# A scan stage on VectorE: partial sums taken up one step later, a sixth buffer for them, and source tiles placed at other points of TensorE's queue

## The chip, the cores and the metric

The kernel runs on one core of a Trainium2 chip. A core has a matrix engine (PE; its weight loads are shown as PEld), a vector engine (DVE), a scalar engine for activations and copies (ACT), a general engine (POOL) and a queue engine that issues transfers (SP). Each works through its own queue in order, and they wait for one another by semaphores. The metric is device time in microseconds (us) of one execution: the median of several runs. A profile is one further execution, recorded instruction by instruction.

## The reference

Two layers work on 4096 tokens of 256 numbers. Layer 0 is a graph convolution with a selective scan (Mamba), followed by a mixture of experts; layer 1 has another graph convolution and another mixture. All is float32. The change lies in the first part of layer 0:

```
h = relu(adj @ layernorm(x) @ gcn_w + gcn_b)
h = layernorm(h) * ln_g + ln_b
xz = h @ w_in;  xc, z = xz[:, :512], xz[:, 512:]
u = silu(causal_conv4(xc) + conv_b)
dbc = u @ w_xp;  dt = softplus(dbc[:, :16] @ w_dt + b_dt)
B, C = dbc[:, 16:32], dbc[:, 32:]
state = exp(dt * A) * state + dt * u * B      # per token; 512 channels x 16 states
y = sum over states of (state * C) + u * D_skip
x = x + (y * silu(z)) @ w_out
```

## The kernel before

**Tiles and steps.** The 4096 tokens are cut into 8 chunks of 512. The 512 channels are 4 blocks (`m`) of 128, one channel to a partition, and the 16 states are taken in pairs (`g`). One step is one block with one pair of states, so a chunk has 32 steps: steps 0 to 15 take blocks 0 and 1 in turn over the 8 pairs, steps 16 to 31 blocks 2 and 3. All 256 steps run in one Python loop (L1195), whose order is written out by hand for PE, DVE, ACT and POOL; SP's order is left to the scheduler.

**One step (class `Step`).** For step n, POOL multiplies dt*u by the broadcast row B into `db` (L1105, 128x1024, both states at once). ACT computes the decay exp(dt*A) for each state into a PSUM tile `da` (L1113, two buffers). DVE scans along the 512 tokens, once for each state (L1120), and multiplies by the row C into `hc` (L1130, 128x1024, five buffers). ACT keeps the last column as the state (L1126). In the next step a transfer on POOL's queue adds the second half of `hc` to the first (`pair`, L1134). Later PE multiplies the sum by the identity and adds it up over the 8 pairs in a PSUM bank `psy` (`total`, L1147; two banks, ps_y). The first sum of a block (g = 0: steps 0, 1, 16 and 17) is preceded by the skip product u*D (L1142, weights `dD`). After the eighth (steps 14, 15, 30 and 31), and in the step after its sum, DVE multiplies `psy` by silu(z) in place of u (`gate`, L1156), which frees the bank. A float32 matmul shows as two instructions in the profile.

**Which sum is taken up when.** The loop at L1234 takes up, in step n, the sum of step n-3, so that the transfer of `hc` has about two steps to land. In the last chunk `hc` is not paired (`paired` is false), PE adds both halves, and the sum of step n-2 is taken up at once.

**What runs beside the scan.** While chunk c is scanned, three things are prepared on PE and ACT.

- `propagation(c+2)` multiplies the adjacency by the normalised x. It is a generator of 66 pieces: for each half of the chunk, 32 pieces (one 128-row tile of x; four matmul instructions of 128x256, L644) into the one PSUM bank `pt`, and a 33rd, in which ACT copies the bank into `pts` (L650) and the next half's first matmul must wait for it. The source tiles `at` come by SP in transfers of four pieces each, with three buffers.
- `Front(c+1)` makes the inputs of the next chunk's scan by a plan of steps (`PLAN`, L660): the GCN product in step 8, the transposes `turn` in 12 (PE, L737), `turned` in 13 (ACT, L744, into `hT`), the in-projection `xz` from 13 on (PE, L756), the causal convolution `conv` as products with diagonal matrices (PE, L773), silu into `us` in 17 and 21 (ACT, L783), the projections, dt and softplus. Entries from 32 on are steps 0 to 7 of the next chunk: the gate half of `xz`, its copy into `zs` (L769) and its silu (L780).
- From step 8 of chunk 6 on there is no propagation left. `Tail` does the out-projection of finished chunks there, with the residual x loaded into `xr` (L883), and `Last` that of chunk 7.

**The planner.** The loop at L1164 to L1174 spreads the 66 pieces over the 32 steps. Each step has an estimated cost on PE and on DVE, and each piece goes to the step where PE's cost less DVE's is smallest. `pieces[i]` is the result; steps 3, 8, 13, 15 to 17, 20 and 23 get none, steps 27 and 29 to 31 five each. The call `advance(pieces[i])` comes at a step's end (L1255). The prologue does chunk 0's propagation and `Front(0)`, with pieces of chunk 1 filled in by the table `FILL`.

In step n the loop issues, in this order: inputs of step n+1 (POOL), the pair transfer of n-1 (POOL), the two scans (DVE) and decays of n+1 (ACT), the product (DVE), the gates of sums taken up in step n-1 (DVE), the sums (PE), the plan's entries, `Tail`, and the pieces. The lines in question:

```
while summed < n - 1 and (summed < n - 2 or not steps[summed].paired):
    steps[summed].total()
    gated.append(summed)
    summed += 1
```

Of the kernel before, what the change touches and what calls it, by code (L numbers as in the profile page):

```python
# [9 lines left out]
F32 = mybir.dt.float32  # L10
# [8 lines left out]
P = 128  # L19
CW = 512  # L20
# [8 lines left out]
def kernel(ctx: ExitStack, tc: tile.TileContext, out: bass.AP, **a):  # L29
    nc = tc.nc  # L30
    x, adj, adjT = a["x"], a["adj"], a["adjT"]
    N, D = x.shape
# [508 lines left out]
    with ExitStack() as s1:  # L541
# [76 lines left out]

        PE_RATIO = 1.0
        FILL = {11: 8, 12: 2, 16: 1, 18: 2, 20: 2, 21: 6, 22: 1, 24: 40}  # L620
        PIECE, PE_STEP, DVE_STEP = 1.0, 1.1, 4.3
        PE_COST = {"gcn": 2, "turn": 0.8, "xz": 2, "conv": 4, "project": 2, "dt": 1}
        DVE_COST = {"biased": 0.8, "stats": 1.4, "soft": 2.7}
# [2 lines left out]
        def propagation(c):  # L626


            halves = psts[c] = []
            for r0 in range(c * CW, c * CW + CW, HW):  # L630
                pt = ps_pt.tile([P, DB, HW], F32, name="pt", tag="pt")
                for j4 in range(NT // 4):
                    at = adp.tile([P, 4, HW], F32, name="at")
                    nc.sync.dma_start(
                        at,
                        adjT[j4 * 4 * P:(j4 + 1) * 4 * P, r0:r0 + HW].rearrange(
                            "(j p) i -> p j i", p=P
                        ),
                    )
                    for jj in range(4):  # L640
                        j = 4 * j4 + jj
                        for k in range(DB):

                            nc.tensor.matmul(  # L644
                                pt[:, k, :], xl[:, j, k * P:(k + 1) * P], at[:, jj, :],
                                start=(j == 0 and k == 0), stop=(j == NT - 1 and k == DB - 1),
                            )
                        yield
                pts = w1p.tile([P, DB, HW], F32, name="pts", bufs=2)
                nc.scalar.copy(pts, pt)  # L650
                halves.append(pts)
                yield

        class Front:

# [3 lines left out]

            PLAN = {  # L660
                8: ["gcn 0", "gcn 1"], 9: ["biased 0", "biased 1"], 11: ["normal"],
                12: ["turn 0", "turn 1"], 13: ["turned 0", "turned 1", "xz 0", "xz 1"],
                14: ["in 0", "in 1", "xz 2"], 15: ["conv 0", "in 2"], 16: ["conv 1"],
                17: ["silu 0", "conv 2"], 18: ["xz 3"], 19: ["in 3", "project 0"],
                20: ["conv 3"], 21: ["silu 1"], 22: ["project 1"],
# [75 lines left out]
            def do_turned(self, k):  # L741
                if k == 0:
                    self.hT = w1p.tile([P, DB, CW], F32, name="hT", tag="hT")
                nc.scalar.activation(  # L744
                    self.hT[:, k, :], self.ps.pop(("turn", k)), AF.Identity,
                    bias=ln_b[:, k:k + 1], scale=ln_g[:, k:k + 1],
                )

            def do_xz(self, m):
                if m == 0:  # L750
# [107 lines left out]
        class Tail:  # L858
# [21 lines left out]
                        tails.pop(0)  # L880

            def fetch(self):
                self.xr = w2p.tile([P, 2, D], F32, name="xr")  # L883
                rows = tokens(x, self.c)[:, 2 * self.hh:2 * self.hh + 2, :]
                nc.sync.dma_start(self.xr, rows)
                if self.kept is None:
                    self.y = fronts[self.c].us[:, :, self.hh * HW:(self.hh + 1) * HW]
                else:
                    self.y = adp.tile([P, 4, HW], F32, name="at")
                    nc.sync.dma_start(self.y, self.kept[:, :, self.hh * HW:(self.hh + 1) * HW])  # L890
# [108 lines left out]
        class Last:  # L999
# [6 lines left out]

            def fetch(self):
                for hh in range(2):
                    t = w2p.tile([P, 2, D], F32, name="xr")
                    nc.sync.dma_start(t, tokens(x, NC - 1)[:, 2 * hh:2 * hh + 2, :])  # L1010
                    self.xr.append(t)

# [22 lines left out]
            def norm(self):  # L1035
# [5 lines left out]
                for hh in range(2):  # L1041
# [20 lines left out]
                    for k in range(DB):  # L1062
                        for j in range(2):
                            nc.tensor.transpose(
                                ps_t[:, k, j * P:(j + 1) * P], xn[:, j, k * P:(k + 1) * P], ident
                            )
                    xT = w1p.tile([P, DB, HW], F32, name="pts", bufs=2)
                    nc.scalar.copy(xT, ps_t)
                    for j in range(2):
                        for k in range(DB):  # L1070
# [10 lines left out]
        class Step:  # L1081
# [43 lines left out]
            def product(self):  # L1125
                nc.scalar.copy(  # L1126
                    state[:, self.m, 2 * self.g:2 * self.g + 2], self.db[:, :, CW - 1]
                )
                self.hc = w2p.tile([P, 2, CW], F32, name="hc", bufs=5)
                nc.vector.tensor_tensor(self.hc, self.db, self.cb, ALU.mult)  # L1130

            def pair(self):
# [25 lines left out]
        with tc.manual_schedule(engines={  # L1158
# [8 lines left out]
                    pe[i % STEPS] += PE_COST.get(name.split()[0], 0.0)  # L1167
                    dve[i % STEPS] += DVE_COST.get(name.split()[0], 0.0)
            pieces = [0] * STEPS
            for _ in range(2 * NT + 2):  # L1170
                i = min(range(STEPS), key=lambda i: pe[i] - PE_RATIO * dve[i])
                pieces[i] += 1
                pe[i] += PIECE
            late = sum(pieces[:8])  # L1174

            def advance(k=1):
                for _ in range(k):
                    next(prop, None)

            prop = propagation(0)  # L1180
            advance(NT + 1)
# [9 lines left out]
                advance(k)  # L1191
                left -= k
            advance(left)
            steps, tails, kept, gated, summed = [], [], {}, [], 0
            for n in range(NC * STEPS):  # L1195
                c, i = divmod(n, STEPS)
                if n == 0:
# [33 lines left out]
                for k in gated:  # L1231
                    steps[k].gate()
                gated = []
                while summed < n - 1 and (summed < n - 2 or not steps[summed].paired):  # L1234
                    steps[summed].total()
                    gated.append(summed)
                    summed += 1
# [5 lines left out]
                if c == NC - 1:  # L1243
# [8 lines left out]
                        last.first(0)  # L1252
                    elif i in (27, 28):
                        last.residual(i - 27)
                advance(pieces[i])  # L1255
                cur = nxt
            n = NC * STEPS
            while summed < n:
# [422 lines left out]
```

## Time and profile before

| What | us |
| --- | --- |
| median of three runs (lowest, highest) | 2462.78 (2461.95, 2464.04) |
| the profiled execution, its own time | 2457.31 |
| its span, first to last instruction | 2455.4 |
| prologue, until the first scan | 168.6 |
| scan stage, chunks 0 to 7 | 137.4, 140.4, 140.2, 139.4, 140.4, 140.2, 145.4, 137.9 |
| after the scan (experts, layer 1) | 1158 |
| granted TensorE clock, mean share | 0.957 |

The lengths of chunks and steps are read from the timeline, from the start of one step's first scan on DVE to that of the next. These are the steps of chunks 0 to 6 that matter, in us:

| Step | chunk 0 | 1 | 2 | 3 | 4 | 5 | 6 |
| --- | --- | --- | --- | --- | --- | --- | --- |
| 1 | 3.63 | 3.68 | 3.68 | 3.68 | 3.68 | 3.68 | 3.68 |
| 2 | 3.63 | 4.29 | 4.28 | 4.28 | 4.28 | 4.29 | 4.29 |
| 8 | 5.41 | 5.41 | 5.76 | 6.04 | 5.41 | 5.41 | 5.86 |
| 18 | 4.29 | 5.80 | 5.62 | 4.29 | 5.79 | 5.59 | 6.12 |
| 19 | 4.66 | 4.66 | 4.67 | 4.66 | 4.66 | 4.66 | 6.45 |
| 20 | 3.62 | 3.62 | 3.62 | 3.62 | 3.62 | 3.62 | 3.63 |
| 22 | 5.41 | 5.54 | 5.54 | 5.40 | 5.54 | 5.54 | 5.40 |

Steps 9 to 11, 26, 27, 29 and 30 are longer than 3.7 us because DVE has work of `Front` in them.

How to read the rows: a row of a timeline gives the start in us, the duration, the engine, the line of the kernel, the operation, what it writes and reads, how many instructions are merged, and in brackets the idle time of that engine before it with what ended it. A row of the waits gives who waited for whom, the total in us, how often, and the longest. Matmuls overlap: the time from one start to the next, not the duration, is what one costs PE. At full rate that is 0.215 us for 256 columns and 0.43 us for 512.

### The profile page before, as it was taken

Reading aid. Unit: us, or ns where it says so; the run is one execution under the profiler, and the core shown is the slowest. Engines: PE = TensorE matmul, PEld = TensorE weight load, DVE = VectorE, ACT = ScalarE, POOL = GpSimd, SP = SyncE. Lnnn points to the kernel's source line nnn. Section 1 sums busy time; section 2 is a strip of 40 time slices with the busy share of each in tenths; the row PEclk is TensorE's granted clock in tenths of the full one; section 3 lists DMA queues with packets and bytes.
Section 4 is the critical chain, followed back from the end, with each engine's and each line's share of the span. In section 5 each row is a group of like instructions: output and inputs, shape, how many; then the busy total and the mean of one; then the engine's idle time right before and its main releaser. Section 6 shows DMA issues by size and latency. Waiting matters only on the chain. (4 is left out here: it accounts for less than half of the span.)

```text
span 2455.4 us, 27712 instructions
## 1 busy us (share of the span) xinstructions
PE 2254.5 (92%) x8984; PEld 1635.0 (67%) x8984; DVE 1656.8 (67%) x2377; ACT 1180.5 (48%) x2013; POOL 1142.7 (47%) x831
## 2 busy tenths in 40 slices
PE   5989989999999999997994999979999999999995
PEld 4765655646565564653563888857788888888874
DVE  4049999999999999999898311155366666754233
ACT  1136657465665646566662322224455555633321
POOL 1027677777777677676560555420000000036652
PEclk9989999999999999997995999989999999999998
DMA  6359998989999998998665777743244444457886
GB/s 206 94 158 247 233 272 224 272 219 266 243 241 273 226 271 221 272 241 214 211 211 159 265 227 234 228 143 112 90 147 148 147 146 146 141 158 230 243 284 238
DMA packets 290956, 509.46 MB, mean 207 GB/s; under 512 B 25312, under 2 KB 157536, under 8 KB 289904
## 3 DMA queue, kind: packets, MB, share of 16 engines
q1 hardware_dynamic: 244528, 410.54, 53.9%
q0 software_dynamic: 46272, 97.03, 18.2%
q8 instruction: 75, 1.23, 0.2%
q14 instruction: 81, 0.66, 0.1%
HBM read 406.03 MB, written 42.73 MB: 183 GB/s over the span
## 5 line engine op out<-in xcount | busy, mean ns | idle before, releaser
L1105 POOL TENSOR_TENSOR db<-du,bb 128x1024 f32<-128x1024 f32 x256 | 606.9, 2371 | 357.9 <-ACT state L1126 129.6
L1120 DVE TENSOR_TENSOR_SCAN db<-da,state,db 128x512 f32<-128x512 f32 x512 | 627.4, 1266 | 44.8 <-ACT da L1113 42.6
L1113 ACT ACTIVATE da<-dt,negA 128x512 f32<-128x512 f32 x512 | 347.7, 691 | 358.6 <-DVE db L1120 356.8
L644 PE MATMUL pt<-at,gn 128*128 128x256 f32 x2048 | 488.1, 391 | 34.0 <-DMA at<-in_adjT_dram 27.1
L644 PEld LDWEIGHTS pt<-at,gn 128*128 128x128 f32 x2048 | 398.7, 196 | 164.0 <-issue 74.2
L1405 PE MATMUL pf<-gn,f 128*128 128x256 f32 x2048 | 452.0, 380 | 0.0
L1405 PEld LDWEIGHTS pf<-gn,f 128*128 128x128 f32 x2048 | 387.1, 190 | 56.7 <-issue 6.4
L1130 DVE TENSOR_TENSOR hc<-db,cb 128x1024 f32<-128x1024 f32 x256 | 331.2, 1294 | 17.9
L1147 PE MATMUL psy<-hc,ident 128*128 128x512 f32 x576 | 303.7, 621 | 42.7 <-DMA hc<-hc 38.9
L79 POOL TENSOR_TENSOR ln_rs<-ln_rs,mhalf 128x4 f32<-128x4 f32 (+1 forms) x25 | 33.3, 1331 | 510.6 <-DVE ln_rs L78 450.7
L460 DVE TENSOR_TENSOR yk<-ps_y,bk 128x512 f32<-128x512 f32 x73 | 50.4, 691 | 316.4 <-PE ps_y L455 293.7
L1394 ACT ACTIVATE f<-f 128x1024 f32<-128x1024 f32 x128 | 134.6, 1057 | 194.0 <-DVE f L1393 129.6
L470 PE MATMUL ps_h<-xkT,wk 128*128 128x256 f32 x864 | 212.9, 388 | 10.8 <-DVE xkT L495 7.6
L455 PE MATMUL ps_y<-wk,hk 128*128 128x256 f32 x864 | 211.1, 381 | 0.1
L1134 POOL DMA_DIRECT2D hc<-hc x224 | 195.0, 871 | 0.2
L1147 PEld LDWEIGHTS psy<-hc,ident 128*128 128x128 f32 x576 | 110.0, 197 | 119.9 <-issue 53.2
L470 PEld LDWEIGHTS ps_h<-xkT,wk 128*128 128x128 f32 x864 | 159.5, 193 | 45.4 <-ACT hk L474 11.6
L1393 DVE TENSOR_SCALAR f<-at 128x1024 f32<-128x1024 f32 x128 | 88.0, 688 | 148.3 <-PE pf L1405 134.9
L455 PEld LDWEIGHTS ps_y<-wk,hk 128*128 128x128 f32 x864 | 161.9, 191 | 21.5 <-ACT hk L474 0.9
L1400 DVE SCALAR_TENSOR_TENSOR cnt<-at,cnt 128x1024 bf16<-128x1024 f32 x120 | 145.9, 1216 | 16.4 <-DMA at<-in_adjT_dram 16.1
L474 ACT ACTIVATE hk<-ps_h,d_b 128x256 f32<-128x256 f32 x140 | 66.0, 473 | 184.2 <-PE ps_h L470 184.2
L756 PE MATMUL ps_xz<-hT,w_in 128*128 128x512 f32 x256 | 126.1, 628 | 14.3 <-ACT hT L744 14.3
(305 smaller groups left out, 2569.6 us busy)
## 6 DMA issues: line engine op xcount, KB each, us to landing
at<-in_adjT_dram SPq DMA_DIRECT2D x256, 512.0 KB, 4.4
bb<-bcd SPq DMA_DIRECT2D x128, 512.0 KB, 5.2
cb<-bcd SPq DMA_DIRECT2D x128, 512.0 KB, 4.9
hc<-hc POOLq DMA_DIRECT2D x224, 256.0 KB, 5.3
wk<-in_L_ffn_W_dram SPq DMA_DIRECT2D x70, 512.0 KB, 5.5
wk<-in_L_ffn_expert_w_dram SPq DMA_DIRECT2D x114, 256.0 KB, 4.3
yg<-d_ys SPq DMA_DIRECT2D x14, 512.0 KB, 4.7
yd<-us SPq DMA_DIRECT2D x6, 1024.0 KB, 7.8
```

What stands on the lines that cost most here:

```text
L455: nc.tensor.matmul(ps[:, j, :], hT[:, m, j * P:(j + 1) * P], w[:, m, :], start=(m == 0), stop=(m == kb_out - 1),)
L470: nc.tensor.matmul(ps[:, j, :], w[:, d, m * P:(m + 1) * P], xT[:, d, :], start=(d == 0), stop=(d == DB - 1),)
L644: nc.tensor.matmul(pt[:, k, :], xl[:, j, k * P:(k + 1) * P], at[:, jj, :], start=(j == 0 and k == 0), stop=(j == NT - 1 and k == DB - 1),)
L1105: nc.gpsimd.tensor_tensor(self.db, self.f.du[self.half][:, self.mi:self.mi + 1, :].to_broadcast([P, 2, CW]), self.bb, ALU.mult,)
L1113: nc.scalar.activation(da, self.f.dt[self.half][:, self.mi, :], AF.Exp, scale=negA[:, self.m, n:n + 1])
L1120: nc.vector.tensor_tensor_scan(self.db[:, j, :], da, self.db[:, j, :], state[:, self.m, n:n + 1], ALU.mult, ALU.add,)
L1130: nc.vector.tensor_tensor(self.hc, self.db, self.cb, ALU.mult)
L1134: nc.gpsimd.dma_start(self.hc[:, 0, :], self.hc[:, 1, :], accum_op=ALU.add)
L1147: nc.tensor.matmul(f.psy[m], ident, self.hc[:, j, :], start=False, stop=(self.g == GS - 1 and j == last),)
L1394: nc.scalar.activation(f, f, AF.Square)
L1400: nc.vector.scalar_tensor_tensor(cnt, at, 0.0, cnt, ALU.is_gt, ALU.add)
L1405: nc.tensor.matmul(pf[:, t, :], f[:, jj, t * P:(t + 1) * P], gn[:, j, :], start=(j == 0 and t % 2 == 0), stop=(j == NT - 1 and t % 2 == 1),)
```

## The change

1. The sum of a paired step is taken up in step n+4 instead of n+3, and `hc` has six buffers.
2. A plan entry `fill` in step 13, between `turned` and `xz`, issues two pieces of the propagation (the table `FILLED`). The planner counts them, so 64 pieces are left to spread. Steps 24 and 25 have one piece fewer each (1 and 2 for 2 and 3); all other steps keep theirs. The entry is also met in the prologue.
3. The 33rd piece, the bank copy, ends a step's pieces: what is left over (`owed`) goes to the next step. The first copy falls in step 28 and one piece moves to step 29; the second is the last piece of step 7.
4. To make room, the residual `xr` of `Tail` and `Last` shares the two buffers of `pts`, and the last chunk's transposed tile uses the buffers of `h` and `hT`.

```
+        FILLED = {13: 2}
...
                 nc.scalar.copy(pts, pt)
                 halves.append(pts)
-                yield
+                yield True
...
-                12: ["turn 0", "turn 1"], 13: ["turned 0", "turned 1", "xz 0", "xz 1"],
+                12: ["turn 0", "turn 1"], 13: ["turned 0", "turned 1", "fill", "xz 0", "xz 1"],
...
+            def do_fill(self):
+
+                advance(FILLED[13])
...
-                self.xr = w2p.tile([P, 2, D], F32, name="xr")
+                self.xr = w1p.tile([P, 2, D], F32, name="xr", tag="pts", bufs=2)
...
-                    t = w2p.tile([P, 2, D], F32, name="xr")
+                    t = w1p.tile([P, 2, D], F32, name="xr", tag="pts", bufs=2)
...
-                    xT = w1p.tile([P, DB, HW], F32, name="pts", bufs=2)
+                    xT = w1p.tile([P, DB, HW], F32, name="xnT7", tag=("h", "hT")[hh])
...
-                self.hc = w2p.tile([P, 2, CW], F32, name="hc", bufs=5)
+                self.hc = w2p.tile([P, 2, CW], F32, name="hc", bufs=6)
...
-            for _ in range(2 * NT + 2):
+            for i, k in FILLED.items():
+                pe[i] += k * PIECE
+            for _ in range(2 * NT + 2 - sum(FILLED.values())):
...
-            def advance(k=1):
-                for _ in range(k):
-                    next(prop, None)
+            def advance(k=1, wait=False):
+
+
+                while k > 0:
+                    k -= 1
+                    if next(prop, None) and wait:
+                        break
+                return k
...
-                while summed < n - 1 and (summed < n - 2 or not steps[summed].paired):
+                while summed < n - 1 and (summed < n - 3 or not steps[summed].paired):
...
-                advance(pieces[i])
+                owed = advance(pieces[i] + owed, True)
+                if i == 7:
+                    while owed:
+                        owed = advance(owed, True)
```

## The prediction, made before the result

> **What bounds the kernel now.** I read the page first, then the busy times of windows cut at the chunks of the scan stage, then the waits of each engine inside 165:1297 us, then the timelines of single steps. The scan stage runs from 165 to 1297 us, 256 steps in 8 chunks of 32, and nothing outside it but the prologue is touched. Two rows of the page (instructions and busy time, mean ns, idle before and its releaser) and two chunks as windows (length, busy time of PE, PEld, DVE, ACT, POOL, granted clock, DMA):
>
> ```profile
> L1120 DVE TENSOR_TENSOR_SCAN db<-da,state,db 128x512 f32<-128x512 f32 x512 | 627.4, 1266 | 44.8 <-ACT da L1113 42.6
> L1147 PE MATMUL psy<-hc,ident 128*128 128x512 f32 x576 | 303.7, 621 | 42.7 <-DMA hc<-hc 38.9
> ```
> ```profile
> 446.40:586.60 140.20, 131.47 (x433) 81.56 (x432) 132.49 (x122) 82.70 (x144) 104.06 (x65) 0.98 0.95 248
> 586.60:726.00 139.40, 131.28 (x428) 81.58 (x427) 133.01 (x122) 83.02 (x144) 104.15 (x65) 0.96 0.95 248
> ```
>
> Of a chunk's 140 us DVE works 132.5 and PE 131.5. A step is two scans and one product on DVE, 3.68 us, of which 0.09 is issue; so the stage is DVE's, and PE's idle time, the 38.9 us for the hc transfers among it, costs only what reaches DVE. The waits inside the stage show the way by which it does:
>
> ```profile
> DVE db L1120 <- ACT da L1113: 42.6, 34, 3.9
> ACT xc L763 <- PE ps_xz L756: 20.7, 22, 4.3
> ACT us L783 <- PE ps_xz L773: 13.8, 12, 1.4
> PE psy L1147 <- DMA hc<-hc: 38.9, 17, 5.8
> PE ps_xz L756 <- ACT hT L744: 14.3, 6, 2.9
> ```
>
> DVE waits for almost nothing but the decays da, and ACT is late with those behind its two table loads for a silu, and behind PE. The timeline gives the places: in chunks 1 to 5 DVE stands still in step 8 (1.7 to 2.2 us), step 18 (1.3 to 1.4; 0.09 in chunks 0 and 3) and step 22 (1.7 to 1.9), and next to nowhere else. PE has no idle time from step 15 to step 27: there it works off a backlog that starts with the in-projection xz. PE at that start in chunk 2, then in chunk 3:
>
> ```profile
> 501.61 1.02 PE L1147 MATMUL psy<-hc,ident 128*128 128x512 f32 x2
> 505.54 4.75 PE L756 MATMUL ps_xz<-hT,w_in 128*128 128x512 f32 x7 [2.91 <-ACT hT L744]
> ```
> ```profile
> 641.56 1.80 PE L644 MATMUL pt<-at,gn 128*128 128x256 f32 x4
> 643.16 1.92 PE L1147 MATMUL psy<-hc,ident 128*128 128x512 f32 x2
> 646.36 3.70 PE L756 MATMUL ps_xz<-hT,w_in 128*128 128x512 f32 x8 [1.29 <-ACT hT L744]
> ```
>
> Both start 4.02 us into step 13. After 2.91 us of idling, chunk 2's first matmuls start 1.01, 0.85 and 0.85 us apart; chunk 3's, after 1.29 us, 0.53 and then 0.43. (Chunk 3 had its half rate earlier: the four matmuls at 641.56 take 1.80 us, elsewhere 1.03.) So the second conv ends 1.48 us later against its step in chunk 2. ACT in step 18 of chunk 2, step 18 of chunk 3, step 22 of chunk 2:
>
> ```profile
> 520.86 0.69 ACT L783 ACTIVATE us<-ps_xz,conv_b 128x512 f32<-128x512 f32 x1
> 522.78 0.69 ACT L783 ACTIVATE us<-ps_xz,conv_b 128x512 f32<-128x512 f32 x1 [1.23 <-PE ps_xz L773]
> 523.48 1.28 ACT L1113 ACT_TABLE_LOAD   x1
> ```
> ```profile
> 661.69 1.26 ACT L783 ACTIVATE us<-ps_xz,conv_b 128x512 f32<-128x512 f32 x2
> 662.97 1.28 ACT L1113 ACT_TABLE_LOAD   x1
> ```
> ```profile
> 540.29 0.69 ACT L783 ACTIVATE us<-ps_xz,conv_b 128x512 f32<-128x512 f32 x1 [1.14 <-PE ps_xz L773]
> ```
>
> Without the wait for PE the chain load, two silus, load, da sets a step of 4.29 us (chunk 3, step 18: 660.77 to 665.05). A gate of 0.69 us fits under it there, to the tenth.
>
> **The change part by part.**
>
> Sums a step later. The 38.9 us of PE waits for hc mostly go: a pair landed 5.3 us after issue (median), 8.0 at most, and gets 3.7 us more. By itself this is worth nothing, because PE then waits at steps 4 and 5 instead, where psy needs the gate of the step before. It moves three things.
> (a) The gates go from steps 2, 3, 18, 19 to 3, 4, 19, 20. At 2 to 4 that is neutral: lengths 4.29, 4.23, 3.63 become 3.68, 4.29, 4.23. At 18 the gate was hidden under ACT's chain, which still sets 4.29, and in step 20 it is paid: 4.23 for 3.62, +0.61 in 7 chunks: +4.3 (in chunk 6 the gate waits for PE's sum in both orders, until the same time). ACT's copy into zs in step 4 then waits for the gate at that step's end (1.2 us), and is done 2.4 us before DVE wants the next decay: nothing.
> (b) The skip product of step 17 (two dD matmuls, 0.43 us apart, 0.86) leaves the queue ahead of the last conv and goes behind it. Conv ends 0.86 earlier and step 22's silu is asked for 0.61 later by (a): 1.47 against waits of 1.00 (chunk 3) to 1.14. Step 22 falls from 5.41, 5.54, 5.54, 5.40, 5.54, 5.54, 5.40 to 4.29: -8.3. Bounds: 0, if something else held conv, to 8.3; PE has no idle there, so I take the whole.
> (c) Step 8: PE finishes the sources some 2 us earlier: it no longer waits at steps 2 and 6 (3.09 and 0.88 us in chunk 2), and about 1.2 us come back at 4 for the gate. ACT's copy of them waited 0.52 and 0.33 us in chunks 3 and 6, whose steps are 6.04 and 5.86 against 5.41: -1.1.
>
> The fill. Two pieces, eight matmuls 0.215 us apart, 1.72 us, go from steps 24 and 25 into the 2.91 us for hT; 1.2 us of idling is left, as in chunks 0 and 3 (1.42, 1.29), whose xz ran at full rate. Step 18 falls from 5.80, 5.62, 5.79, 5.59 in chunks 1, 2, 4, 5 to 4.29: -5.6. But PE, no longer paced by hc, will idle about 3 us before the transposes, and may run the piece, the sum and the fill after them at half rate, as chunk 3 did. Half rate lasted 3.1 to 5.2 us in the rows (1061.8, 179.0): xz then starts 0.2 to 1.2 us late, against 0.2 us that chunk 3's second silu had to spare. Bounds for step 18: -5.6 to about 0; I take 0.1 us a chunk off in six: -5.0. The source tiles are asked for two pieces sooner; PE waited for none in this stage, three buffers hold 12 pieces, and steps 9 to 12 use 13: covered.
>
> The skill's "TensorE: Matmul & The Clock Gate", Part 1, puts the drop to half rate after an idle window of about 3.4 us, in windows that run freely. By that, 2.91 us should not cool PE, the fill would buy nothing at step 18 and the sum would be -1.6; here 2.91 us was followed by half rate in all four chunks, and 3.09 us (at 455.77) was not. I go by the rows.
>
> Pieces kept off the bank copy. The first copy falls in step 28, where one piece moves to 29; the waits are 6.3 us over six places, in steps where PE catches up anyway: 0. Prologue: PE works without a gap there, so xz comes 1.72 us later, but ACT then stands 11.17 us at the copy of the sources (150.10), for which two pieces fewer remain: 0, at most +1.7.
>
> xr in pts' buffers. The first loads, which before were issued at 22.9 us, must wait for chunk 7's GCN products (1044 us) on SP's queue; PE's residual matmul at 1046.1 may wait 1 to 2 us, with 2.6 us of PE idling in step 10 as cover: 0. POOL's queue keeps its order. The last chunk's transposed tile takes the buffers h and hT, whose last use is over by then.
>
> Chunk 7, where sums are not paired. The new rule puts the sums of 223, 224 and 225 into one step, ahead of xz 4 on PE, and the sum of 224 needs the bank that the gate of 222 frees, now one step later:
>
> ```profile
> 1161.04 1.10 PE L1147 MATMUL psy<-hc,ident 128*128 128x512 f32 x2 [0.96 <-DMA hc<-hc]
> 1165.63 2.08 PE L1142 MATMUL psy<-us,dD 128*128 128x512 f32 x2 [3.49 <-DVE us L1156]
> 1170.83 1.02 PE L1142 MATMUL psy<-us,dD 128*128 128x512 f32 x2
> 1173.40 1.02 PE L756 MATMUL ps_xz<-hT,w_in 128*128 128x512 f32 x2
> ```
>
> That gate ends at 1165.58; moved, at 1169.05 (step 2 without it, 5.56, then 4.22). From 1165.63 to 1173.40 and on to 1191 PE has no gap, and DVE waits for it by way of ACT (1.3, 4.0 and 0.5 us in steps 5 to 7). So +3.5, all of it on the path; between 0, if PE's half rate ends sooner, and 5.2, a second half-rate spell.
>
> Sum: 4.3 - 8.3 - 1.1 - 5.0 + 3.5 = -6.6 us. The profiled execution took 2457.31 us, span 2455.4; that would give 2450.7. The median of the three runs is 2462.78, 5.5 above it, so 2456.2 there.
>
> **The rivals.**
> 1. The fill buys nothing at step 18: it runs at half rate, or xz does still. For it: chunk 3's 1.80 us; against it: its xz was fast. Step 18's -5.0 goes: -1.6, 2461.2.
> 2. xr blocks SP: if the queue stands at xr until 1044, bb for steps 10 and 11 lands some 5.2 us later, db takes 2.35, and the scan of 1048.2 starts near 1052: +3.9, so -2.7, 2460.1. Against it: SP's order is not the program's (xr at 22.9 us).
> 3. Slower: xz is pushed out far past hT by the fill, at half rate with all before it. A delay of 3 us makes step 18 some 2.8 us longer than 4.29, 7.1 against 4.29 to 5.80, in six chunks: 42.5 us for 31.4, +11.2 in place of -5.0, together +9.6, 2472.4. It decides from a delay of about 2.2 us on (the sum then reaches +4.9); the half-rate spells seen give 1.2.
> 4. Chunk 7's stall is absorbed and xz starts on time: -10.7, 2452.1.
>
> **How the numbers follow.** Chances: forecast 0.48, rivals 0.22, 0.10, 0.12, 0.08. The forecast's own range is 2453 to 2460, its terms a half off. The range of 2451.5 to 2465 takes in all but rival 3 and a little. A change under 0.2% (4.9 us) can't be told from none: faster is below 2457.9, which is four fifths of the forecast case, rival 4 and a little of the others, 0.50; slower is rival 3 and surprises, 0.14; the rest 0.36.
>
> **What would show it.** Right: PE's wait for hc below 10 us; xz of chunks 1 to 5 starting 0.43 us apart; steps 18 and 22 at 4.3, step 20 at 4.2; DVE's wait for da from 42.6 to about 32, with steps 5 to 7 of chunk 7 longer by 3.5. Wrong: silus that still wait for conv, xz starting later than 4.6 us into step 13, a POOL db waiting for bb in chunk 6.

## The result, and the profile after

The changed kernel takes 2458.99 us (median of 12 runs, 2453.91 to 2462.58) against 2461.73 us for the kernel before, run beside it (12 runs): a ratio of 0.9987 with a 95% interval of 0.9975 to 1.0000. The forecast, 2456.2 against 2462.78, was a ratio of 0.9973: the sign was right, but only about half of the gain arrived (3.2 us by the ratio, for 6.6), and the interval reaches up to no change at all. The run e1 below, with the same kernel, has an interval that lies below 1. The profiled execution took 2459.77 us, span 2457.9, and so was not shorter than the profiled one of before (2457.31, span 2455.4). Cut into parts, the two spans say where to look (the part behind the scan is counted here from the end of the last scan, in the table ahead of the prediction from 1297 us):

| Part of the span, us | before | after |
| --- | --- | --- |
| prologue, until the first scan | 168.6 | 166.4 |
| scan stage | 1121.1 | 1115.8 |
| behind the scan | 1165.7 | 1175.7 |
| chunks 0 to 7 | 137.4, 140.4, 140.2, 139.4, 140.4, 140.2, 145.4, 137.8 | 136.8, 138.3, 139.4, 138.3, 138.3, 138.3, 144.8, 141.5 |

The scan stage became 5.3 us shorter, of the 6.6 that were forecast. The part behind it, which the prediction left out as untouched, became 10.0 us longer in this execution.

The two rows of the page that carried the prediction, now of the kernel after (instructions, busy time, mean ns, idle time before them and its releaser). The wait for `hc` has gone from PE's row, and DVE's wait for `da` has fallen by less than five us:

```profile
L1125 DVE TENSOR_TENSOR_SCAN db<-da,state,db 128x512 f32<-128x512 f32 x512 | 627.5, 1267 | 40.1 <-ACT da L1118 37.9
L1152 PE MATMUL psy<-hc,ident 128*128 128x512 f32 x576 | 304.2, 625 | 9.1 <-DMA hc<-hc 8.2
```

Chunks 2 and 3 as windows (length, busy time of PE, PEld, DVE, ACT, POOL, granted clock, DMA). DVE still works 132.8 us of each; only its standing still became less:

```profile
441.60:581.00 139.40, 131.49 (x432) 81.30 (x432) 132.78 (x121) 82.74 (x144) 104.07 (x65) 0.98 0.96 249
581.00:719.30 138.30, 132.78 (x434) 82.47 (x433) 132.85 (x122) 82.61 (x144) 104.18 (x65) 0.96 0.95 252
```

The waits of the stage in the kernel after. ACT's wait for the second conv (`us`, 13.8 us before) is nearly gone; a wait of PE for the gates has come, as part (a) had it, and the longest of them, 7.4 us, is chunk 7's:

```profile
DVE db L1125 <- ACT da L1118: 37.9, 37, 4.9
PE psy L1147 <- DVE us L1161: 15.2, 7, 7.4
PE psy L1152 <- DMA hc<-hc: 8.2, 7, 3.6
ACT xc L768 <- PE ps_xz L761: 15.0, 16, 5.1
ACT us L788 <- PE ps_xz L778: 1.8, 2, 1.1
```

The in-projection in PE's timeline, chunk 1 and then chunk 2. No idle time is left ahead of it, and it runs at full rate in both. But PE stood still for 2.6 us before the transposes, and what follows these ran at half rate in both: four matmuls of a piece take 1.88 us for 1.03. In chunk 1 the full rate came back with the first matmuls of the fill (the eight take 1.76 us, from 360.98 to 362.74), and xz starts 4.36 us into step 13. In chunk 2 the transposes were at half rate too, the full rate came back only after three matmuls of the fill (the eight take 2.28 us), and xz starts 5.44 us in:

```profile
355.52 0.33 PE L738 MATMUL ps_turn<-ident,h 128*128 128x128 f32 x1 [2.57 <-ACT h L730]
...
357.60 1.88 PE L645 MATMUL pt<-at,gn 128*128 128x256 f32 x4
359.27 1.91 PE L1152 MATMUL psy<-hc,ident 128*128 128x512 f32 x2
360.98 1.93 PE L645 MATMUL pt<-at,gn 128*128 128x256 f32 x8
362.74 3.60 PE L761 MATMUL ps_xz<-hT,w_in 128*128 128x512 f32 x8
```
```profile
496.45 1.91 PE L645 MATMUL pt<-at,gn 128*128 128x256 f32 x4
498.16 1.92 PE L1152 MATMUL psy<-hc,ident 128*128 128x512 f32 x2
499.87 2.45 PE L645 MATMUL pt<-at,gn 128*128 128x256 f32 x8
502.15 2.31 PE L761 MATMUL ps_xz<-hT,w_in 128*128 128x512 f32 x5
```

ACT in the kernel after: step 18 of chunk 1, where the two silus run together and the step is 4.38 us; step 18 of chunk 2, where the late xz leaves the second silu waiting, 5.46 us; and step 22 of chunk 1, 4.35 us, with no wait for conv left:

```profile
377.73 1.36 ACT L788 ACTIVATE us<-ps_xz,conv_b 128x512 f32<-128x512 f32 x2
379.11 1.28 ACT L1118 ACT_TABLE_LOAD   x1
```
```profile
516.06 0.69 ACT L788 ACTIVATE us<-ps_xz,conv_b 128x512 f32<-128x512 f32 x1
517.81 0.69 ACT L788 ACTIVATE us<-ps_xz,conv_b 128x512 f32<-128x512 f32 x1 [1.06 <-PE ps_xz L778]
518.52 1.28 ACT L1118 ACT_TABLE_LOAD   x1
```
```profile
394.68 1.27 ACT L788 ACTIVATE us<-ps_xz,conv_b 128x512 f32<-128x512 f32 x2
395.96 1.28 ACT L1118 ACT_TABLE_LOAD   x1
```

Chunk 7 in PE's timeline. The sum of step 224 waits for the gate of step 222, and xz starts at 1165.85, 25.2 us into the chunk, where it started 21.5 us into it before:

```profile
1158.08 2.08 PE L1147 MATMUL psy<-us,dD 128*128 128x512 f32 x2 [7.39 <-DVE us L1161]
...
1165.85 3.60 PE L761 MATMUL ps_xz<-hT,w_in 128*128 128x512 f32 x8
```

### The profile page after: what moved, and what is told of

It is laid out like the page before. It is cut to its first block, busy times and chain, and to the rows that moved or that the text cites. A ratio compares the mean times of both kernels' runs of the same rounds, so it can differ in the third digit from the quotient of the medians.

```text
span 2457.9 us, 27675 instructions
## 1 busy us (share of the span) xinstructions
PE 2257.0 (92%) x8984; PEld 1637.2 (67%) x8984; DVE 1657.4 (67%) x2377; ACT 1180.0 (48%) x2013; POOL 1142.7 (46%) x831
## 5 line engine op out<-in xcount | busy, mean ns | idle before, releaser
L1125 DVE TENSOR_TENSOR_SCAN db<-da,state,db 128x512 f32<-128x512 f32 x512 | 627.5, 1267 | 40.1 <-ACT da L1118 37.9
L460 DVE TENSOR_TENSOR yk<-ps_y,bk 128x512 f32<-128x512 f32 x73 | 50.5, 691 | 325.0 <-PE ps_y L455 282.4
L1409 ACT ACTIVATE f<-f 128x1024 f32<-128x1024 f32 x128 | 134.6, 1057 | 201.1 <-DVE f L1408 136.3
L1408 DVE TENSOR_SCALAR f<-at 128x1024 f32<-128x1024 f32 x128 | 88.2, 689 | 151.0 <-PE pf L1420 137.9
L1410 ACT ACTIVATE f<-f 128x1024 f32<-128x1024 f32 x128 | 134.5, 1055 | 3.4
```

Source lines behind the costliest of these rows:

```text
L1125: nc.vector.tensor_tensor_scan(self.db[:, j, :], da, self.db[:, j, :], state[:, self.m, n:n + 1], ALU.mult, ALU.add,)
L1409: nc.scalar.activation(f, f, AF.Square)
```

## The experiments

The theory after the result was: the scan stage does what was forecast, and the moved buffers alter the order of the instructions behind the scan, which costs some us there. The rivals were: the lost gain is measurement, or it is lost in the stage itself. The runs came on three chips, whose medians for the kernel before are 2460.3, 2480.0 and 2458.7 us; ratios are therefore always to the kernel before on the same chip, with a 95% interval. Each run is of 12 executions, e8 of 7 and e12 of 6. "Stage" is the scan stage in the run's profile.

| Run | chip | ratio [95%] | stage | step 20 | step 22 (chunks 0 to 5) | chunk 7 | order behind the scan |
| --- | --- | --- | --- | --- | --- | --- | --- |
| before, given profile | | | 1121.1 | 3.62 | 5.40 to 5.54 | 137.8 | of before |
| after, given profile | | 0.9987 [0.9975, 1.0000] | 1115.8 | 4.22 | 4.35 | 141.5 | new |
| e1 after again | A | 0.9982 [0.9973, 0.9992] | 1113.7 | 4.22 | 4.35 | 140.6 | new |
| e2 room only | A | 1.0026 [1.0016, 1.0036] | 1120.5 | 3.62 | 5.45 to 5.59 | 137.9 | new |
| e3 fill only | A | 0.9984 [0.9974, 0.9994] | 1115.4 | 3.62 | 5.40 to 5.54 | 138.0 | of before |
| e4 later sums only | A | 1.0004 [0.9993, 1.0016] | 1119.5 | 4.22 | 4.35 | 140.7 | new |
| e5 order back | B | 0.9977 [0.9962, 0.9991] | 1114.2 | 4.22 | 4.35 | 140.6 | of before |
| e6 chunk 7 | B | 0.9976 [0.9962, 0.9989] | 1110.3 | 4.22 | 4.35 | 136.5 | new |
| e7 gates back | B | 0.9990 [0.9975, 1.0005] | 1114.1 | 3.62 | 4.59 to 4.74 | 140.2 | new |
| e8 all three | B | 0.9945 [0.9925, 0.9965] | 1109.6 | 3.62 | 4.59 to 4.74 | 137.0 | of before |
| e9 before again | C | 1.0006 [0.9992, 1.0020] | 1120.8 | 3.62 | 5.40 to 5.54 | 137.8 | of before |
| e10 one sum | C | 0.9990 [0.9978, 1.0002] | 1118.6 | 3.62 | 4.36 | 137.2 | of before |
| e11 one sum, fill | C | 0.9964 [0.9952, 0.9977] | 1112.8 | 3.62 | 4.36 | 137.0 | of before |
| e12 all three again | C | 0.9955 [0.9937, 0.9973] | 1110.0 | 3.62 | 4.60 to 4.74 | 136.5 | of before |

"Order" is that of the instructions in each engine's queue behind the scan stage, read from the programs: there are just two, the one of the kernel before and that of the kernel after.

**e1: the changed kernel again.** No edit.

> The changed kernel once more, with a second profile. If the work behind the scan stage is slower by its order (theory A), the time from the last scan to the end is again near 1175.7 us, 10 us above the 1165.7 of the kernel before; if it was chance of one execution (theory B), it comes back towards 1166 to 1170. Scan stage, first scan to last: 1115.8 us again under both. Ratio 0.997 to 1.000.

Ratio 0.9982, stage 1113.7. Five of the chunks take 138.2 or 138.3 us, as chunks 1 and 3 to 5 of the first profile did; chunk 2 is 138.2 here and has no late xz (4.02 us into step 13), so its 139.4 was chance. The stage gain is 7.3 us, measured against the mean of the two profiles of before (1121.0), and the whole program gains 4.4. Behind the scan it is 1173.1 us, nearer to the 1175.7 of theory A than to the 1166 to 1170 of the rival, but by itself no proof.

**e2: the room alone.** The six buffers and the moved tiles stay; the fill, the kept-off bank copy and the later sums are taken out:

```
-        FILLED = {13: 2}
+        FILLED = {}
-                12: ["turn 0", "turn 1"], 13: ["turned 0", "turned 1", "fill", "xz 0", "xz 1"],
+                12: ["turn 0", "turn 1"], 13: ["turned 0", "turned 1", "xz 0", "xz 1"],
-                while summed < n - 1 and (summed < n - 3 or not steps[summed].paired):
+                while summed < n - 1 and (summed < n - 2 or not steps[summed].paired):
-                owed = advance(pieces[i] + owed, True)
+                owed = advance(pieces[i] + owed)
```

> Only the room is made (xr in the buffers of pts, the last chunk's tile in h and hT, six hc buffers); sums, pieces and plan as in the kernel before. Scan stage as before, 1121 us, under both theories. Theory A: the instructions behind the scan stand in the order of the changed kernel, so 5 to 10 us are lost there: ratio 1.002 to 1.004. Theory B: ratio 1.000 within 0.001.

Ratio 1.0026 with an interval that lies above 1: slower by some 6 us, with a stage of 1120.5 us, as before. So the room costs time, and it costs it outside the stage. That speaks for the theory and against both rivals.

**e3: the fill alone.** The buffers and the sums as before, the fill and the kept-off bank copy as after:

```
-                self.xr = w1p.tile([P, 2, D], F32, name="xr", tag="pts", bufs=2)
+                self.xr = w2p.tile([P, 2, D], F32, name="xr")
-                    t = w1p.tile([P, 2, D], F32, name="xr", tag="pts", bufs=2)
+                    t = w2p.tile([P, 2, D], F32, name="xr")
-                    xT = w1p.tile([P, DB, HW], F32, name="xnT7", tag=("h", "hT")[hh])
+                    xT = w1p.tile([P, DB, HW], F32, name="pts", bufs=2)
-                self.hc = w2p.tile([P, 2, CW], F32, name="hc", bufs=6)
+                self.hc = w2p.tile([P, 2, CW], F32, name="hc", bufs=5)
-                while summed < n - 1 and (summed < n - 3 or not steps[summed].paired):
+                while summed < n - 1 and (summed < n - 2 or not steps[summed].paired):
```

> Only the fill and the pieces kept off the bank copy, with the buffers and the sums of the kernel before; the work behind the scan stands in the order of the kernel before. Step 18 of chunks 1, 2, 4 and 5 falls to 4.3 us, step 22 stays at 5.4, step 20 at 3.62, chunk 7 as before: scan stage 1115 us (-6). Theory A: behind the scan 1166 us, so the whole gain shows, ratio 0.997 to 0.998. Theory B: the same stage, behind the scan anything from 1166 to 1176.

Ratio 0.9984, the same as the whole change; stage 1115.4, which is 5.6 below before, against the 5.0 forecast for the fill. Step 18 takes 4.29 to 4.39 us in all of chunks 0 to 5. The fill works by itself. Behind the scan this execution took 1170.4 us where 1166 was expected: single executions of one order differ by several us there.

**e4: the later sums alone.** The kernel after without the fill and without the kept-off bank copy (the first, second and last pair of lines of e2's diff).

> The later sum and the room, without fill and without pieces kept off the copy. Step 20 4.22 us, step 22 4.35, chunk 7 141.5 us as in the changed kernel. Without the fill PE idles before the in-projection: if that cools it, step 18 of chunks 1, 2, 4 and 5 stays at 5.6 to 5.8 and the stage takes about 1120 us; if the half rate before the transposes is over by then, 4.4 and 1115. Theory A: behind the scan as in the changed kernel, ratio 1.001 to 1.003; theory B: 0.998 to 1.000.

Ratio 1.0004, stage 1119.5: 1.5 us less than before, where the sum of (a), (b), (c) and chunk 7 was -1.6. Steps 20 and 22 are those of the kernel after, and chunk 7 takes 140.7 us. Step 18 is at 5.67 to 5.80 us in chunks 0 to 3 and at 4.29 in 4 and 5: four of six at half rate as in the kernel before, but other ones. The ratio lies between what the theory (1.001 to 1.003) and the rival (0.998 to 1.000) asked for, and its interval reaches both.

**e5: the order back.** The kernel after, but the last chunk's result goes to memory through an `hc` buffer and not through `xr`:

```
+                put = w2p.tile([P, 2, CW], F32, name="hc", bufs=6)
...
-                    after(nc.scalar.copy(self.xr[hh], self.ps[hh]), done)
+                    to = put[:, hh, :].rearrange("p (j d) -> p j d", j=2)
+                    after(nc.scalar.copy(to, self.ps[hh]), done)
...
-                    nc.sync.dma_start(rows, self.xr[hh])
+                    nc.sync.dma_start(rows, to)
```

> The changed kernel, but the last chunk's result is put into x1d by way of a buffer of hc instead of xr. With that the instructions behind the scan stand, on PE, DVE, POOL, SP and ACT, in the order of the kernel before. Scan stage as in the changed kernel, 1114 to 1116 us. Theory A (the order behind the scan costs the change 4 to 7 us): the time behind the scan falls from 1173 to 1178 to 1166 to 1170, ratio 0.995 to 0.997. Theory B (the place of xr or chance, not the order): behind the scan 1173 to 1176 again, ratio 0.998.

This one edit brings back the order of before on every engine. Ratio 0.9977, above the 0.995 to 0.997 expected, with an interval that overlaps those of the kernel after; by this run's time alone the gain is not resolved, and the 1166 to 1170 us expected behind the scan can't be read on this chip (1192.9 us, see the last section). What the edit does show is that this one use of `xr` decides the order. How the order costs time can be seen in the two given profiles, in the place where the orders differ most. There the first of 32 equal expert tiles run beside the source tiles of layer 1 (`propagate1`: a transfer `at`, then `f` on DVE, then two activations of `f` on ACT). In the timeline of ACT, and then of PE, the kernel before:

```profile
1369.73 1.05 ACT L1394 ACTIVATE f<-f 128x1024 f32<-128x1024 f32 x1
...
1376.29 1.06 ACT L1394 ACTIVATE f<-f 128x1024 f32<-128x1024 f32 x1 [3.46 <-DVE f L1393]
1377.26 0.45 ACT L474 ACTIVATE hk<-ps_h,d_b 128x256 f32<-128x256 f32 x1
```
```profile
1377.76 1.13 PE L470 MATMUL ps_h<-xkT,wk 128*128 128x256 f32 x4 [0.25 <-ACT hk L474]
```

And the kernel after, ACT, DVE, PE:

```profile
1369.09 1.06 ACT L1409 ACTIVATE f<-f 128x1024 f32<-128x1024 f32 x1 [4.22 <-DVE f L1408]
...
1380.36 1.06 ACT L1409 ACTIVATE f<-f 128x1024 f32<-128x1024 f32 x1 [5.89 <-DVE f L1408]
1381.32 0.46 ACT L474 ACTIVATE hk<-ps_h,d_b 128x256 f32<-128x256 f32 x1
```
```profile
1379.63 0.69 DVE L1408 TENSOR_SCALAR f<-at 128x1024 f32<-128x1024 f32 x1 [3.57 <-DMA at<-in_adjT_dram]
```
```profile
1381.83 2.07 PE L470 MATMUL ps_h<-xkT,wk 128*128 128x256 f32 x4 [3.63 <-ACT hk L474]
```

In the new order the first source tile is taken up 8.8 to 10.7 us after the first expert tile, where it was 2.2 to 2.3 us, and more of them stand close together. At the fourth expert tile ACT has an activation of `f` queued ahead of `hk`. Its source has not landed, ACT stands still for 5.89 us, PE waits 3.63 us for `hk` and then runs at half rate (four matmuls in 1.86 us, 1381.83 to 1383.69). From the third expert tile's result (the end of DVE's last instruction for the tile, L460) to the fourth's it takes 7.2 to 7.4 us in seven of the eight profiles with the order of before and 8.9 in the eighth, which is e5's; in the six with the new order it is 10.9 to 13.3. From the scan's end to the eighth result:

| Order | Profiles | us to the eighth result | mean |
| --- | --- | --- | --- |
| of before | before, e3, e5, e8, e9, e10, e11, e12 | 130.4, 132.4, 133.9, 132.3, 130.6, 130.9, 130.5, 130.3 | 131.4 |
| new | after, e1, e2, e4, e6, e7 | 135.6, 133.8, 133.1, 137.6, 137.6, 136.3 | 135.7 |

To the last product of layer 1's propagation the means are 899.7 and 904.6 us, without overlap (897.4 to 902.1 and 902.4 to 906.5). The four profiles e9 to e12 were taken after the two ranges had been put down in the expectation of e9. The tiles themselves lie as in the kernel after in e5, e8 and e10 to e12, but for this one use; so it is not their place alone that costs time.

**e6: chunk 7 as before.** The kernel after, but the sums from the last four steps of chunk 6 on are taken up as in the kernel before:

```
-                while summed < n - 1 and (summed < n - 3 or not steps[summed].paired):
+                while summed < n - 1 and (summed < n - (2 if summed >= NC * STEPS - STEPS - 4 else 3) or not steps[summed].paired):
```

> The changed kernel, with the sums of the last four steps of chunk 6 taken up as before. If the +3.7 us of chunk 7 come from the sum of step 224 that waits for the gate of 222 (forecast), chunk 7 goes from 141 us back to 138, PE's first in-projection of chunk 7 stands 21.5 us after its start instead of 25.3, and all other chunks stay; ratio about 0.0014 below the changed kernel. If something else delays chunk 7 (xr on SP's queue), it stays at 141.

Ratio 0.9976, stage 1110.3. Chunk 7 falls from about 141 to 136.5 us. The sum of step 224 now waits 3.96 us for the gate instead of 7.39, and xz follows it sooner; PE's timeline of this kernel:

```profile
1154.07 2.08 PE L1147 MATMUL psy<-us,dD 128*128 128x512 f32 x2 [3.96 <-DVE us L1161]
...
1162.12 3.60 PE L761 MATMUL ps_xz<-hT,w_in 128*128 128x512 f32 x8
```

That is step 5 of the chunk: 8.60 us in the kernel after, 7.73 in e1, 5.25 here. A further 1.4 us of the fall lies in steps 17 and 18, and e7, which leaves the start of chunk 7 alone, has that too, so it need not come from the edit. The gate of step 222 was the cause of the wait, and at the start of the last chunk the later sums cost what was forecast, with nothing to show for it.

**e7: the gates back in steps 18 and 19.** The kernel after, but the sums of steps 14 and 15 are taken up as in the kernel before:

```
-                while summed < n - 1 and (summed < n - 3 or not steps[summed].paired):
+                while summed < n - 1 and (summed < n - (2 if steps[summed].i in (14, 15) else 3) or not steps[summed].paired):
```

> The changed kernel, with the sums of steps 14 and 15 taken up as before, so that these two gates go back to steps 18 and 19. If a gate is hidden under ACT's chain in step 18 (forecast), step 18 stays at 4.3 to 4.4 us, step 20 falls from 4.22 to 3.62, and chunks 0 to 5 shorten by 0.6 us each: stage 3.6 to 4 us shorter. If the gate adds to step 18 as well, step 18 becomes 4.9 and nothing is gained.

Ratio 0.9990 [0.9975, 1.0005], stage 1114.1. Step 20 falls by 0.60 to 3.62 us, as the working of (a) has it, but step 22 rises by 0.25 to 0.39, because it is asked for earlier and the last conv is not ready. ACT in step 22 of chunk 1 of this kernel:

```profile
396.47 0.69 ACT L788 ACTIVATE us<-ps_xz,conv_b 128x512 f32<-128x512 f32 x1 [0.28 <-PE ps_xz L778]
```

So about 0.3 us a chunk is left of 0.6. The stage did not become 3.6 to 4 us shorter, as expected: it is 1.7 below the given profile of after and 0.4 above e1's, because besides the rise of step 22, step 18 was long here in chunks 1 and 4 (5.08 and 5.43 us) and step 26 in chunk 3 (by 1.18). The prediction's 1.47 us against a wait of 1.00 to 1.14 had this in it: without the 0.61 of (a) only 0.86 remain.

**e8: all three.** The edits of e5, e6 and e7 together.

> The three edits together: order behind the scan, chunk 7 and the gates. Scan stage 1107 us by their sum (1114 - 3.7 - 3.6), behind the scan 1166 to 1170 by theory A: ratio 0.993 to 0.995, faster than both kernels. By theory B 0.996.

Ratio 0.9945 [0.9925, 0.9965], stage 1109.6, for the 1107 expected. By the ratio that is about 14 us faster than before, by the medians 10.5, more than any of the three edits gives alone. The ratio is in the theory's range (0.993 to 0.995), but the interval takes in the rival's 0.996.

**e9: the kernel before again.** No edit.

> The kernel before, unchanged, as a second profile and a comparison with itself: ratio 1.000 within 0.0015. Theory A (behind the scan the order of the instructions decides): from the end of the scan to the eighth expert tile 130 to 134 us, and to the end of layer 1's propagation 898 to 902 us, as in the kernels with this order so far, not the 134 to 138 and 902 to 907 of the kernels with the other order. Theory B (those differences are from one execution to another): anywhere between. Half rate at xz: if it is a matter of the execution, other chunks than 1, 2, 4 and 5 have step 18 above 5.5 us; if it is fixed by the 2.91 us of idling, the same four.

Ratio 1.0006 to itself, stage 1120.8, and the order-bound times as expected (130.6 and 899.5 us). Step 18 is long in chunks 1, 3 and 4 here (5.64, 5.81, 5.66) and at 4.29 in chunks 0, 2 and 5, against 1, 2, 4 and 5 in the given profile. Two lines of PE's timeline, chunk 1 and chunk 2 of this one execution, have the same 2.91 us of idling and opposite ends: three matmuls in 2.93 us, and seven in 3.27:

```profile
361.49 2.93 PE L756 MATMUL ps_xz<-hT,w_in 128*128 128x512 f32 x3 [2.91 <-ACT hT L744]
```
```profile
502.14 3.27 PE L756 MATMUL ps_xz<-hT,w_in 128*128 128x512 f32 x7 [2.91 <-ACT hT L744]
```

**e10: one sum later.** No fill; only the sum of step 17, with the skip product ahead of it, is taken up a step later, and e5's edit is in:

```
-                while summed < n - 1 and (summed < n - 3 or not steps[summed].paired):
+                while summed < n - 1 and (summed < n - (3 if steps[summed].i == 17 else 2) or not steps[summed].paired):
```

> Without the fill and the kept-off bank copy; only the sum of step 17, with its skip product and the sums queued behind it, one step later, all others as before; six buffers, and the last result put through an hc buffer, so that the order behind the scan is that of before. Theory: step 22 falls from 5.4-5.54 to 4.35-4.7 us in chunks 0 to 6, step 20 stays at 3.62, chunk 7 at 138, so the stage is 6 to 8 us shorter; step 18 stays at 4.3 or 5.6 to 5.8 by the half rate. Ratio 0.9965 to 0.9975. Rival (step 22 needs all sums a step later, gates too): step 22 stays above 5.2, ratio 0.999 to 1.001.

Ratio 0.9990 [0.9978, 1.0002], stage 1118.6: half a miss. Step 22 is 4.36 us with step 20 at 3.62, so it needs neither the other sums nor the moved gates; the rival is out. But this edit takes more off the queue than (b) does: as the other sums keep their steps, both the skip product and the sum of step 17, 0.86 us each, go behind the last conv, and 1.72 us is more than the waits of 1.00 to 1.14. The skip product alone leaves 0.25 to 0.39 us of wait, as e7 showed. The stage gains only 2.4 us for 6 to 8. Over chunks 0 to 6, step 25 grew by 2.3 us in all against e9's: two sums come together in step 21, and the next product on PE's queue, on which ACT's copy `dbc` waits, starts later. And step 8 takes 5.77 to 7.44 us in chunks 1 to 6, where the kernels with all sums later have 5.41 everywhere. In chunk 1 ACT waits there for the sources that PE adds up, which is what (c) is about:

```profile
340.38 0.59 ACT L651 COPY pts<-pt 128x512 f32<-128x512 f32 x1 [1.76 <-PE pt L645]
```

**e11: one sum later, and the fill.** e10 with the fill and the kept-off bank copy of the kernel after.

> The same with the fill and the bank copy at the end of a step's pieces. Theory: as the run before, and step 18 at 4.3 to 4.4 in five or six of chunks 0 to 5, another 3 to 6 us: stage 1108 to 1111 us, ratio 0.994 to 0.996, the same as the kernel with the three edits. Rival (the sums later at other steps are worth something too): stage 1112 or more.

Ratio 0.9964 [0.9952, 0.9977], inside the expected range at its upper end; stage 1112.8, above the 1108 to 1111 expected, and by that measure the rival held: sums later at other steps are worth something, some 3 us beside e12. They lie in steps 5 to 9, which together take 3.1 us more here than in e12 over chunks 0 to 6. Step 18 is 4.30 to 4.40 in five chunks and 5.41 in chunk 3, where xz started 5.38 us in.

**e12: all three again.** The kernel of e8.

> The kernel with the three edits again: stage 1109 to 1111 us, ratio 0.994 to 0.996. If the order behind the scan counts, scan end to the eighth expert tile 130 to 134 us.

Ratio 0.9955 [0.9937, 0.9973], stage 1110.0, 130.3 us to the eighth result. So this kernel is faster than both the one before and the changed one, on two chips: about 11 to 14 us below before by the ratios, where the change as it was made gave 3 to 4.

**Time and stage set against each other.** For each run the change in time (ratio less one, times the median of before on that chip) less the change of its stage (against 1121.0) is what the rest of the program added. With the new order it is +2.0 (after), +2.9 (e1), +6.9 (e2), +2.5 (e4), +4.7 (e6) and +4.4 (e7), mean +3.9 us. With the order of before it is +1.7 (e3), +1.1 (e5), -2.2 (e8), -0.1 (e10), -0.7 (e11) and -0.1 (e12), mean 0.0. Each of these carries an interval of 2.5 to 5 us, and its stage comes from one execution; only the two groups can be told apart, by about 4 us. They differ on each chip that had both: means of +4.1 and +1.7 us on A, +4.6 and -0.6 on B. That is the gain that went missing.

## Why the prediction was right, and where it was wrong

The sign and the range held, and 2458.99 us is 2.8 us from the forecast. By itself this says little: the range of 2451.5 to 2465 us takes in no change as well, and the measured change is below the 0.2% which the prediction could not tell from none. The terms inside the stage say more. They are, from the steps of the two given profiles:

| Step of the prediction | forecast, us | profile after less before |
| --- | --- | --- |
| (a) gates: step 20 | +4.3 | +4.2 |
| (b) skip product: step 22 | -8.3 | -7.9 |
| (c) step 8 | -1.1 | -1.1 (with step 9) |
| fill: step 18 of chunks 1, 2, 4, 5 | -5.0 | -4.3 |
| chunk 7 | +3.5 | +3.7 |
| everything else in the stage | 0 | +0.1 |
| prologue | 0, at most +1.7 | -2.2 |
| behind the scan | 0 | +10.0 |

**The failed step is "xr in pts' buffers ... 0", with "nothing outside it but the prologue is touched" ahead of it.** I looked for the cost of the moved tiles where they are used, in the waits for their buffers, and there it was nothing: SP issued the first `xr` load at 1030 us without holding up a B or C row, and a wait of PE for it (4.9 us) cost nothing that can be seen (chunk 6 takes 145.5 us in e2, with the moved loads, and 145.4 before). Rival 2, which was about that queue, did not come. But the work behind the scan is ordered by the scheduler, and with the moved tiles it chose another one. The group means put that at about 4 us, and e5's one edit takes the order back. How the place or the release of these buffers leads the scheduler to that order was not tried. Not all of the 10.0 us in the two given profiles is this: the kernel before took 1165.7 us behind the scan in one profile and 1170.6 in the other.

**(a) and (b)** were right in place and size; step 22 ends at 4.35 and not 4.29, and step 21 gives 0.06 us. e7 shows that the two hang together as the working had it: the skip product gives 0.86 us and the late gate 0.6, and the first alone is not enough for the wait. One sign did not come: DVE's wait for `da` fell to 37.9 us and not to about 32. It did not fit the prediction's own sum either. DVE's work stays the same, so its waits can fall only by what the stage gets shorter, 6.6 us in the forecast. The gate that left step 18 leaves DVE idle there: 0.52 us ahead of the next step's scan in chunks 0 and 3, where it was 0.09 before.

**(c)** is as a rule worth more than I took. Against the given profile of before it was -1.1, but step 8 has 2.9 us above 5.41 in e9 and more in e2 and e10, and 5.41 in every chunk but the last wherever the sums are later. Over steps 5 to 9 of chunks 0 to 6 those kernels (after, e1, e4 to e8 and e12) all take 151.7 us; before, e2, e3, e9, e10 and e11 take 1.0 to 6.2 us more. Which chunks are long is a matter of the execution.

**The fill.** The mechanism was right: with the fill no xz of chunks 0 to 5 starts at half rate, and e3 alone gives 5.6 us in the stage. The place of the danger was right too, since in chunk 2 the transposes, the piece, the sum and the first three matmuls of the fill ran at half rate. But "all four chunks" was one draw. Over the five profiles without the fill, 14 of 30 chunks (0 to 5) have a short step 18, 4.4 us or less; with the fill it is 46 of 54 in nine profiles. In the eight others, xz started 5.0 to 5.5 us into step 13, beyond the 4.6 that the prediction named as a sign against it: 1.0 to 1.4 us late, about its bound of 1.2, and short of the 2.2 us from which rival 3 decides. In all eight the half rate began in the transposes and reached one to four matmuls into the fill. Rival 1 is out. The size was part luck: what step 18 takes above 4.29 us adds up, over chunks 0 to 5, to 4.65 us in the mean profile without the fill and to 1.08 in the mean one with it, so the fill is worth about 3.6 us there and not 5.0. And the 3.1 us that the prediction read as the shortest spell of half rate (1061.8) is the end of a longer one: the four transposes before it, from 1060.94 on, are already 0.21 us apart for the 0.11 of full rate.

**Chunk 7** was right, and e6 shows the cause; rival 4, which had it absorbed, is out (its -10.7 is 0.6 more than the sum without the 3.5 us, which gives -10.1).

**The prologue** was 165.0 and 168.6 us in the two profiles of before and 166.0 to 168.5 in those with the fill. The fill's 1.72 us cannot be seen in that.

## What to carry to other kernels

To move a buffer can be to move instructions far away that a scheduler places by it: compare the order of the whole program, not only the stage that was edited, before such a move is costed at nothing. A rule such as "one step later" is several changes at once; go through every place where the rule makes something different, the last chunk's among them, and keep it where it pays. And a rate that depends on what ran a few microseconds ago has to be read from several executions before it is made a term of a sum.

## What the runs showed of the hardware

**Idling and the half rate.** In the profiles without the fill there are 18 in-projections that start after 2.9 us of idling. In 15 the rate was halved (spacings of 0.85 us, in e10 only from the third matmul on), in 3 it was full (0.43), in the same kernel and even the same execution (e9's two lines above). After 1.2 to 1.7 us of idling it was always full, but in one chunk of e4 it was halved after 0.65 us, with other idling just before it. So the length of the last gap does not decide alone. The Trainium skill, "TensorE: Matmul & The Clock Gate", Part 1, speaks of windows of about 3.4 us that run freely, by which the same kernel comes out differently from one run to the next. The differences between executions agree with that. Its idle window of about 3.4 us, read as a threshold for a single gap, does not: 2.9 us was enough more often than not.

**Chips.** The same kernel before has medians of 2460.3, 2480.0 and 2458.7 us on three chips, a spread of 0.9%, several times the effect of the change. On the slow one the extra time lies behind layer 1's propagation, which ends there as soon after the scan as on the others (901.3 to 906.5 us): the part behind the scan takes 1191.7 to 1197.9 us there and 1165.7 to 1177.9 on the others.
